# Layer 0's values products in half-block batches, with results held back and value copies moved to ScalarE

## Chip, cores, metric

One core of one Trainium2 chip. The metric is the device time of one launch in microseconds (us), as the median of several runs. Every run in this document is fast, which means that none was over 1.5% above the fastest of the same kernel. Where two kernels are compared by a ratio, it is the mean time of one kernel's fast runs over that of the other's of the same rounds, so it is not quite the ratio of the medians quoted.

## The reference

Two attention layers over eight images of 64 channels and 64 x 64 positions (4,096 positions an image), in fp32.

```python
# layer 0: f and g have 8 channels, h has 64
s = einsum('bci,bcj->bij', f, g);  beta = softmax(s, axis=2)
x = x + einsum('bcj,bij->bci', h, beta)
# layer 1: group norm, then q, k, v of 64 channels
attn = softmax(q @ k.T * 64**-0.5);  x = proj(attn @ v) + x
```

Scores are never stored whole. For each chunk of columns the kernel makes scores, takes their exponentials, multiplies them with the values, keeps the running sum of the exponentials, and divides at the end.

## The kernel before

Each image has four column chunks (`NC`) and sixteen row tiles (`NT`) per chunk in each layer. The order of work is: layer 0 of images 0 and 1 (here "the start"), then layer 1 of image 0, layer 0 of image 2, layer 1 of image 1, and so on. A layer-0 stretch after the start is called a steady phase here; there are six.

PSUM is eight banks of 512 columns. Two of them (0 and 7) take turns as the accumulator of the values products; the other six, and the accumulator's twin while it is free, hold scores. So a layer-0 step works on six or seven score banks:

```python
# one step of layer 0 (cut)
room = list(range(1, 7))
if closed == 0 and taken != BANK:
    room = sorted(room + [free])          # the seventh bank
...
for (k, t, p, h), bank in group:          # TensorE: scores, one bank each
    seq[k][0].scores(banks[:, bank, :], t, p, h, seq[k][1])
...                                       # ScalarE: exponentials, up to four banks each
new += [(k, 2*t + p, e) for ... if h == 1]   # a block: two banks
...
# ended():
for u in due: u[2]()                      # projections, sums, value copies that are due
for r in ready: weigh(*r, now)            # TensorE: values products of the step BEFORE
ready = new
```

A block (`weigh` of layer 0) is two fp32 products of 512 columns into two halves of one bank; each product is two instructions, so a block is four. After every second block, VectorE adds the exponentials to a running sum (`esum`, 2,048 columns, 2.29 us). At a chunk's end come three pieces of work: `sums` (TensorE sums the running sum over partitions, ScalarE copies it, transfers deal it out as `zt`), `reciprocals` (VectorE, then transfers through DRAM to `r`), and `result` (VectorE multiplies by `r`, adds the residual, takes statistics).

Of the kernel before, what the change touches and what calls it, by code (L numbers as in the profile page):

```python
# [19 lines left out]
CW = 512  # L20
# [48 lines left out]
def fast_path(  # L69
# [19 lines left out]
    nc = tc.nc  # L89
    B, C, N = x.shape  # L90
    C8 = WfT.shape[1]
    NH = N // 2
    NC = NH // CW
    NT = NH // P
# [16 lines left out]
    outer = (0, 7)  # L111
    turn = 0
    lent = None

    def pair():
        nonlocal turn
        if lent is not None:
            return pairs[lent]
        turn += 1
        return pairs[turn % 3]  # L120
# [15 lines left out]
    def matmul(*args, **kwargs):  # L136
        in_order(nc.tensor.matmul(*args, **kwargs))  # L137
# [139 lines left out]
    class Attention:  # L277
# [8 lines left out]
        def values(self, src, w, c):  # L286

            ps = pair()
            for t in range(TPC):
                for m in range(2):  # L290
                    for h in range(2):
                        matmul(
                            ps[ts(m, C), h, ts(t, C)], src[ts(h, C), ds(t * P + m * C, C)],
                            w[ts(h, C), :], start=True, stop=True,
                        )
            self.copy_values(  # L296
                self.vt[:, :, ts(c, TPC), :],
                ps[:, :, 0 : TPC * C].rearrange("k p (t c) -> k p t c", c=C),
            )
# [70 lines left out]

    class Layer0(Attention):
        kind = 0
        copy_values = staticmethod(nc.vector.tensor_copy)
        scale = 1.0
        banks = 1

# [62 lines left out]
                ps, self.g[rows, ts(t, P)], self.f[rows, ts(c, CW)], start=True, stop=True  # L439
            )  # L440

        def weigh(self, acc, e, t, p, start, stop):
            for h in range(2):
                matmul(
                    acc[0][ts(h, C), :], self.vt[:, p, t, :], e[:, h, :], start=start, stop=stop
                )

        def total(self, raw, acc):
# [6 lines left out]

    class Layer1(Attention):
        kind = 1
        copy_values = staticmethod(nc.vector.tensor_copy)
        scale = C**-0.5
        banks = 2  # L460

# [93 lines left out]
                        self.parts[ts(h, C), h, ts(c, CW)], start=True, stop=True,  # L555
                    )

        def weigh(self, acc, e, t, p, start, stop):
            for m in range(2):
                for h in range(2):  # L560
                    matmul(
                        acc[m][ts(h, C), :], self.vt[ts(m, C), p, t, :], e[ts(m, C), h, :],
                        start=start, stop=stop,
                    )

        def total(self, raw, acc):
# [19 lines left out]
    seq = [(at, c) for at in order for c in range(NC)]  # L586
# [5 lines left out]
    def at_step(s, work_, takes=PAIR):  # L592
        nonlocal count
        later.append((s, count, work_, takes))
        later.sort(key=lambda u: u[:2])
        count += 1

    def take(s):

        due, taken = [], 0  # L600
        for u in [u for u in later if u[0] <= s]:
            if not (u[3] and taken):
                due.append(u)
                later.remove(u)
                taken = taken or u[3]
        return due, taken
# [9 lines left out]
    for i, at in enumerate(order):  # L616
        if i > 0:

            where = max(k for k in range(i) if order[k].kind == 1 or k == min(i, 2) - 1)
            for s, u, buffer in at.before():  # L620
                at_step(where * NC * NT + s, u, buffer)

    ready = []
    acc = esum = first = None

    def weigh(i, j, e, now):
        nonlocal acc, esum, first
        at, c = seq[i]
        t, p = divmod(j, 2)
        n = f"{at.name}_{c}"  # L630
        if j == 0:
            acc = [banks[:, outer[(c + m) % 2 if at.kind == 0 else m], :] for m in range(at.banks)]
            esum = work.tile([P, 2, 2, CW], F32, tag="esum", name=f"esum_{n}")
        at.weigh(acc, e[:, p], t, p, j == 0, j == 2 * NT - 1)
        if p == 0:
            return
        if t == 0:
            first = e
        else:
            nc.vector.tensor_add(esum, first if t == 1 else esum, e)  # L640
        if t == NT - 1:
            finished(i, now)

    def finished(i, now):

        nonlocal closed
        at, c = seq[i]
        closed = max(closed, 1)
        next_kind = seq[i + 1][0].kind if i + 1 < len(seq) else 1
        works = at.finish(acc, esum, c, i)  # L650
        if len(works) == 1:
            at_step(now, works[0])
            return
        sums, reciprocals, result = works
        delay = 7 if at.kind == 0 else 5
        if at.kind == 1 and c == NC - 2 and i + 2 < len(seq) and seq[i + 2][0].kind == 0:
            delay = NT
        spare = None
        if next_kind == 0:

            spare = outer[c % 2 if at.kind == 0 else 1]
        if at.kind == 1 and c < NC - 1:
            spare = None
        at_step(now + delay, lambda: sums(spare), PAIR if spare is None else BANK)

        layer1 = (i // NC + 1) * NC * NT
        if at.kind == 0 and at.b > 0 and c < NC - 1:
            when = layer1 + 1 + 2 * c
            steps = (when, when + 3)
        else:  # L670

            wait = 4 if next_kind == 0 else 3
            steps = (now + delay + wait, now + delay + 2 * wait)
        at_step(steps[0], reciprocals, 0)
        at_step(steps[1], result, 0)

    closed = 1

    def ended():

        nonlocal ready, closed
        closed = max(closed - 1, 0)
        for u in due:
            u[2]()
            if u[3] == BANK:
                closed = 1
        for r in ready:
            weigh(*r, now)
        ready = new

    i = 0
    while i < len(seq):
        at, c = seq[i]
        if at.kind == 1:
            for j in range(0, 2 * NT, 2):
                now = i * NT + j // 2
                due, taken = take(now)
                t = j // 2
                new = []
                both_ps = [pair(), pair()]  # L700
                for p in range(2):
                    at.scores(both_ps[p], t, p, c)
                e = ppool.tile([P, 2, 2, CW], F32, tag="e", name=f"e_{at.name}_{c}_{t}")
                for p in range(2):
                    nc.scalar.activation(e[:, p], both_ps[p], AF.Exp, scale=at.scale)  # L705
                    new.append((i, j + p, e))
                ended()
            i += 1
            continue

        last = next(k for k in range(i, len(seq) + 1) if k == len(seq) or seq[k][0].kind == 1)
        units = [
            (k, t, p, h)
            for k in range(i, last) for t in range(NT) for p in range(2) for h in range(2)
        ]
        u = 0
        while u < len(units):
            k, t = units[u][:2]
            now = k * NT + t
            due, taken = take(now + 1)  # L720
            if any(j == 0 for _, j, _ in ready):
                closed = max(closed, 1)
            free = outer[1]
            if ready:
                free = outer[(ready[-1][0] + 1) % 2]
                if seq[ready[-1][0]][0].kind == 1:
                    closed = 1
            room = list(range(1, 7))
            if closed == 0 and taken != BANK:
                room = sorted(room + [free])  # L730
            if taken == PAIR:
                lent = 0 if room[-1] == 7 else 2
                room = [r for r in room if r not in (2 * lent + 1, 2 * lent + 2)]
            group = list(zip(units[u : u + len(room)], room))
            u += len(group)
            for (k, t, p, h), bank in group:
                seq[k][0].scores(banks[:, bank, :], t, p, h, seq[k][1])
            new = []
            while group:
                (k, t, p, h), bank = group[0]  # L740
                first_ = 2 * p + h
                n_ = min(4 - first_, len(group))
                at, c = seq[k]
                if first_ == 0:
                    e = ppool.tile([P, 2, 2, CW], F32, tag="e", name=f"e_{at.name}_{c}_{t}")
                nc.scalar.activation(  # L746
                    e.rearrange("k p h n -> k (p h) n")[:, first_ : first_ + n_, :],
                    banks[:, bank : bank + n_, :], AF.Exp, scale=at.scale,
                )
                new += [(k, 2 * t + p, e) for (k, t, p, h), _ in group[:n_] if h == 1]  # L750
                group = group[n_:]
            ended()
            lent = None
        i = last
    now = len(seq) * NT
    for r in ready:
        weigh(*r, now)
# [408 lines left out]
```

## Time and profile before

| | before |
|---|---|
| median of the three runs given with the kernel | 3125.45 us (3122.25 to 3125.78) |
| busy in the trace | TensorE 98%, VectorE 80%, ScalarE 65% |
| from the second layer-0 step to layer 1 of image 0 ("the start") | 326.5 us |
| a steady layer-0 phase, all six | 153.0 us |
| a layer-1 phase, the first six | 229.4 to 229.7 us |
| the rest (layer 1 of images 6 and 7, and the end) | 468.9 us |

The lower four rows are differences between starts of score batches in the trace, each phase cut at the second step of layer 1 and the first of layer 0. TensorE is the engine to follow. Its busy share tells little, because a stalled score batch counts as busy until its last bank is free (0.97 us in place of 0.73 in the timeline that the prediction shows); the lengths of steps tell more.

### The profile page before, as it was taken

Reading aid. Unit: us, or ns where it says so; the run is one execution under the profiler, and the core shown is the slowest. Engines: PE = TensorE matmul, PEld = TensorE weight load, DVE = VectorE, ACT = ScalarE, POOL = GpSimd, SP = SyncE. Lnnn points to the kernel's source line nnn. Section 1 sums busy time; section 2 is a strip of 40 time slices with the busy share of each in tenths; the row PEclk is TensorE's granted clock in tenths of the full one; section 3 lists DMA queues with packets and bytes.
Section 4 is the critical chain, followed back from the end, with each engine's and each line's share of the span. In section 5 each row is a group of like instructions: output and inputs, shape, how many; then the busy total and the mean of one; then the engine's idle time right before and its main releaser. Section 6 shows DMA issues by size and latency. Waiting matters only on the chain.

```text
span 3120.9 us, 58240 instructions
## 1 busy us (share of the span) xinstructions
PE 3070.0 (98%) x25523; PEld 1140.2 (37%) x25523; DVE 2504.3 (80%) x1624; ACT 2042.1 (65%) x1957; POOL 16.5 (1%) x41
## 2 busy tenths in 40 slices
PE   7999999999999999999999999999999999999998
PEld 2332334433344333433334333343333433333433
DVE  6998777798768987689776897769977699776676
ACT  5787655686557865578655785557855588555554
POOL 2000000000000000000000000000000000000000
PEclk9999999999999999999999999999999999999999
DMA  3000010100101001010010100101001000000000
GB/s 84 22 8 18 12 35 18 31 8 8 39 15 32 8 8 39 18 28 8 8 39 18 28 8 8 40 17 32 8 13 40 8 18 8 5 22 15 12 11 12
DMA packets 61814, 63.12 MB, mean 20 GB/s; under 512 B 34944, under 2 KB 35024, under 8 KB 61552
## 3 DMA queue, kind: packets, MB, share of 16 engines
q1 hardware_dynamic: 60432, 59.16, 7.6%
q8 instruction: 202, 3.31, 0.4%
q14 instruction: 60, 0.49, 0.1%
q0 software_dynamic: 800, 0.15, 0.0%
q10 hardware_dynamic: 320, 0.01, 0.0%
HBM read 25.06 MB, written 8.65 MB: 11 GB/s over the span
## 4 chain that ended last, share of the span: by engine, by line
PE 92%; DVE 4%; ACT 2%; issue 1%; DMA 1%; SPq 0%; ACTq 0%; DVEq 0%
PE banks L137 92%; DVE esum_l L640 3%; ACT e_l L746 1%; ACT e_l L705 0%; DMA r_l<-recips 0%; DMA w<-in_WgT_dram 0%; DMA fg_l<-high_l 0%; DVE v_l L296 0%; SPq L334 0%; DVE vt_l L296 0%; DMA zt_l<-zs_l 0%; DVE r_l L359 0%; SPq L431 0%; DMA recips<-stash 0%; DVE high_l L421 0%
## 5 line engine op out<-in xcount | busy, mean ns | idle before, releaser
L640 DVE TENSOR_TENSOR esum_l<-esum_l,e_l 128x2048 f32<-128x2048 f32 x896 | 2051.0, 2289 | 394.1 <-ACT e_l L705 338.4
L705 ACT ACTIVATE e_l<-banks 128x1024 f32<-128x1024 f32 x1024 | 992.9, 1021 | 795.6 <-PE banks L137 763.0
L746 ACT ACTIVATE e_l<-banks 128x2048 f32<-128x2048 f32 (+3 forms) x757 | 954.9, 1325 | 233.2 <-PE banks L137 226.5
L137 PE MATMUL banks<-e_l,v_l 64*64 64x512 f32 (+1 forms) x8704 | 1105.0, 591 | 0.0
L137 PE MATMUL banks<-kq_l 64*64 64x512 f32 (+1 forms) x8448 | 1016.2, 586 | 10.3 <-DVE v_l L296 6.0
L137 PE MATMUL banks<-e_l,vt_l 128*64 128x512 f32 x3584 | 831.6, 601 | 0.7
L137 PEld LDWEIGHTS banks<-e_l,v_l 64*64 64x64 f32 (+1 forms) x8704 | 377.7, 133 | 557.2 <-issue 518.6
L137 PEld LDWEIGHTS banks<-kq_l 64*64 64x64 f32 (+1 forms) x8448 | 367.1, 135 | 576.9 <-issue 522.4
L137 PEld LDWEIGHTS banks<-e_l,vt_l 128*64 128x64 f32 x3584 | 233.0, 136 | 459.0 <-issue 455.3
L137 PE MATMUL banks<-fg_l 32*128 32x512 f32 x1792 | 223.3, 469 | 12.0 <-ACT e_l L746 4.6
L137 PEld LDWEIGHTS banks<-fg_l 32*128 32x128 f32 x1792 | 93.2, 183 | 256.5 <-ACT e_l L746 172.3
L640 DVE TENSOR_TENSOR esum_l<-e_l,e_l 128x2048 f32<-128x2048 f32 x64 | 146.1, 2283 | 22.1 <-ACT e_l L746 12.7
L364 DVE TENSOR_TENSOR raw_l<-raw_l,r_l 128x512 f32<-128x512 f32 x64 | 44.0, 688 | 74.4 <-DMA r_l<-recips 74.4
L137 PE MATMUL banks<-esum_l,ones 128*32 128x512 f32 (+2 forms) x508 | 55.0, 500 | 4.3 <-DVE esum_l L310 2.7
L567 DVE COPY raw_l<-banks 128x512 f32<-128x512 f32 x32 | 22.1, 691 | 33.4 <-PE banks L137 33.4
L345 DVE RECIPROCAL stash<-zt_l 128x8 f32<-128x8 f32 x63 | 12.7, 201 | 40.4 <-DMA zt_l<-zs_l 39.6
L541 ACT ACTIVATE kq_l<-banks,qkb 128x512 f32<-128x512 f32 x64 | 40.6, 696 | 0.0
L310 DVE TENSOR_TENSOR esum_l<-esum_l 128x1024 f32<-128x1024 f32 x32 | 38.9, 1215 | 0.0
L137 PE MATMUL banks<-xn_l,wqk 64*64 64x512 f32 x256 | 33.9, 592 | 0.0
L449 ACT COPY raw_l<-banks 128x512 f32<-128x512 f32 x32 | 19.0, 594 | 19.0 <-PE banks L137 19.0
L329 ACT COPY zs_l<-banks 128x512 f32<-128x512 f32 (+1 forms) x63 | 30.9, 490 | 0.0
L296 DVE COPY v_l<-banks 128x512 f32<-128x512 f32 x36 | 24.7, 686 | 6.6 <-PE banks L137 6.5
(88 smaller groups left out, 387.2 us busy)
## 6 DMA issues: line engine op xcount, KB each, us to landing
r_l<-recips SPq DMA_DIRECT2D x126, 128.0 KB, 2.9
fg_l<-high_l SPq DMA_DIRECT2D x224, 64.0 KB, 2.0
x<-in_x_dram SPq DMA_DIRECT2D x32, 256.0 KB, 4.9
kq_l<-kq_l SPq DMA_DIRECT2D x64, 128.0 KB, 2.3
out_dram<-raw_l SPq DMA_DIRECT2D x64, 128.0 KB, 2.5
kq_l<-high_l SPq DMA_DIRECT2D x32, 64.0 KB, 2.0
zt_l<-zs_l SPq DMA_DIRECT2D x128, 2.0 KB, 1.8
zt_l<-zs_l SPq DMA_DIRECT2D x124, 1.0 KB, 1.7
```

What stands on the lines that cost most here:

```text
L137: in_order(nc.tensor.matmul(*args, **kwargs))
L296: self.copy_values(self.vt[:, :, ts(c, TPC), :], ps[:, :, 0 : TPC * C].rearrange("k p (t c) -> k p t c", c=C),)
L310: nc.vector.tensor_add(esum[:, 0], esum[:, 0], esum[:, 1])
L329: nc.scalar.copy(zs, z[:, 0:width])
L345: nc.vector.reciprocal(rt, zh)
L364: nc.vector.tensor_mul(raw, raw, r)
L449: nc.scalar.copy(raw, acc[0])
L541: nc.scalar.activation(self.parts[:, h, cols], ps[:, h, :], AF.Identity, bias=k1["qkb"][:, h : h + 1],)
L567: nc.vector.tensor_copy(raw, acc[0])
L640: nc.vector.tensor_add(esum, first if t == 1 else esum, e)
L705: nc.scalar.activation(e[:, p], both_ps[p], AF.Exp, scale=at.scale)
L746: nc.scalar.activation(e.rearrange("k p h n -> k (p h) n")[:, first_ : first_ + n_, :], banks[:, bank : bank + n_, :], AF.Exp, scale=at.scale,
```

## The change

The intent: let each layer-0 batch hold exactly as much values work as seven score banks call for (three and a half blocks), stop VectorE from standing in front of TensorE, and hold layer-0 results until layer 1, where VectorE has time. The title's "held" did not exist in effect before: the program asked for it, but the scheduler pulled the ready work forward.

```diff
-            self.copy_values(                      # VectorE
+            copy = nc.vector.tensor_copy if lent is None else nc.scalar.copy
+            copy(                                  # ScalarE inside layer 0
...
+    def due_part(ready):
+        room, now_, left = 7, [], []
+        for k, j, e, cols in ready:
+            size = (cols.stop - cols.start) // (CW // 2)      # half blocks
+            if seq[k][0].kind == 1 or room >= size:
+                now_.append((k, j, e, cols)); room -= size
+            elif room == 1 and 0 < j < 2 * NT - 1:            # split by columns
+                mid = (cols.start + cols.stop) // 2
+                now_.append((k, j, e, slice(cols.start, mid)))
+                left.append((k, j, e, slice(mid, cols.stop)))
+                room = 0
+            else: ...
...
-        if at.kind == 1 and c == NC - 2 and i + 2 < len(seq) and seq[i + 2][0].kind == 0:
-            delay = NT                             # third chunk's sums wait for layer 0
...
+        def behind(work_):
+            def made():
+                with tc.issue_after(added):        # behind the last running-sum add
+                    work_()
+            return made
-        at_step(steps[0], reciprocals, 0)
-        at_step(steps[1], result, 0)
+        at_step(steps[0], behind(reciprocals), 0)
+        at_step(steps[1], behind(result), 0)
...
-        for r in ready:
+        for r in batch:
             weigh(*r, now)
-        ready = new
+        ready = left + new
```

(Shortened, and cut: the column slice passed through `weigh`, and the test that closes the seventh bank, which now looks at the batch.)

More of the change, by code (lines that the diff above doesn't have):

```diff
@@ L372, in fast_path @@
         kind = 0
-        copy_values = staticmethod(nc.vector.tensor_copy)
         scale = 1.0
@@ L440, in scores, with weigh @@
             )
-        def weigh(self, acc, e, t, p, start, stop):
+        def weigh(self, acc, e, t, p, start, stop, cols):
             for h in range(2):
                 matmul(
-                    acc[0][ts(h, C), :], self.vt[:, p, t, :], e[:, h, :], start=start, stop=stop
+                    acc[0][ts(h, C), cols], self.vt[:, p, t, :], e[:, h, cols],
+                    start=start, stop=stop,
                 )
@@ L457, in fast_path @@
         kind = 1
-        copy_values = staticmethod(nc.vector.tensor_copy)
         scale = C**-0.5
@@ L556, in scores, with weigh @@
                     )
-        def weigh(self, acc, e, t, p, start, stop):
+        def weigh(self, acc, e, t, p, start, stop, cols):
             for m in range(2):
@@ L561, in weigh @@
                     matmul(
-                        acc[m][ts(h, C), :], self.vt[ts(m, C), p, t, :], e[ts(m, C), h, :],
-                        start=start, stop=stop,
+                        acc[m][ts(h, C), cols], self.vt[ts(m, C), p, t, :],
+                        e[ts(m, C), h, cols], start=start, stop=stop,
                     )
@@ L624, in fast_path, with weigh @@
     acc = esum = first = None
-    def weigh(i, j, e, now):
-        nonlocal acc, esum, first
+    added = None
+    def due_part(ready):
[3 more added lines that the diff above has]
+            if seq[k][0].kind == 1 or room >= size:
+                now_.append((k, j, e, cols))
+                room -= size
+            elif room == 1 and 0 < j < 2 * NT - 1:
[3 more added lines that the diff above has]
+                room = 0
+            else:
+                left.append((k, j, e, cols))
+                room = 0
+        return now_, left
+    def weigh(i, j, e, cols, now):
+        nonlocal acc, esum, first, added
         at, c = seq[i]
@@ L630, in weigh @@
         n = f"{at.name}_{c}"
-        if j == 0:
+        if j == 0 and cols.start == 0:
             acc = [banks[:, outer[(c + m) % 2 if at.kind == 0 else m], :] for m in range(at.banks)]
             esum = work.tile([P, 2, 2, CW], F32, tag="esum", name=f"esum_{n}")
-        at.weigh(acc, e[:, p], t, p, j == 0, j == 2 * NT - 1)
-        if p == 0:
+        at.weigh(acc, e[:, p], t, p, j == 0, j == 2 * NT - 1, cols)
+        if p == 0 or cols.stop < CW:
             return
@@ L639, in weigh @@
         else:
-            nc.vector.tensor_add(esum, first if t == 1 else esum, e)
+            added = nc.vector.tensor_add(esum, first if t == 1 else esum, e).ins
         if t == NT - 1:
@@ L697, in fast_path @@
                 due, taken = take(now)
+                batch, left = ready, []
                 t = j // 2
@@ L705, in fast_path @@
                     nc.scalar.activation(e[:, p], both_ps[p], AF.Exp, scale=at.scale)
-                    new.append((i, j + p, e))
+                    new.append((i, j + p, e, slice(0, CW)))
                 ended()
@@ L720, in fast_path @@
             due, taken = take(now + 1)
-            if any(j == 0 for _, j, _ in ready):
-                closed = max(closed, 1)
+            batch, left = due_part(ready)
             free = outer[1]
-            if ready:
-                free = outer[(ready[-1][0] + 1) % 2]
-                if seq[ready[-1][0]][0].kind == 1:
-                    closed = 1
+            if batch:
+                free = outer[(batch[-1][0] + 1) % 2]
+                if seq[batch[-1][0]][0].kind == 1 or any(b[1] == 0 for b in batch):
+                    closed = max(closed, 1)
             room = list(range(1, 7))
@@ L749, in fast_path @@
                 )
-                new += [(k, 2 * t + p, e) for (k, t, p, h), _ in group[:n_] if h == 1]
+                new += [
+                    (k, 2 * t + p, e, slice(0, CW)) for (k, t, p, h), _ in group[:n_] if h == 1
+                ]
                 group = group[n_:]
```

## The prediction

> **What bounds the kernel now.** I read the page first: busy shares, then the chain that ended last.
>
> ```profile
> PE 3070.0 (98%) x25523; PEld 1140.2 (37%) x25523; DVE 2504.3 (80%) x1624; ACT 2042.1 (65%) x1957; POOL 16.5 (1%) x41
> ...
> PE 92%; DVE 4%; ACT 2%; issue 1%; DMA 1%; SPq 0%; ACTq 0%; DVEq 0%
> ```
>
> TensorE carries 92% of the chain, and the other 8% (some 250 us) is partly start, end and semaphore hops. So the question is only how much TensorE waiting the change can remove. The change touches layer 0, so I next read the timeline of a steady layer-0 stretch, by engine (start, length, group).
>
> ```profile
> 614.49 0.98 PE L137 MATMUL banks<-fg_l 32*128 32x512 f32 x7
> 615.40 3.65 PE L137 MATMUL banks<-e_l,vt_l 128*64 128x512 f32 x16
> ...
> 618.98 0.73 PE L137 MATMUL banks<-fg_l 32*128 32x512 f32 x7
> 619.56 3.23 ACT L746 ACTIVATE e_l<-banks 128x1536 f32<-128x1536 f32 x2 [1.22 <-PE banks L137]
> 619.65 2.80 PE L137 MATMUL banks<-e_l,vt_l 128*64 128x512 f32 x12
> 622.37 0.97 PE L137 MATMUL banks<-fg_l 32*128 32x512 f32 x7
> 623.28 3.65 PE L137 MATMUL banks<-e_l,vt_l 128*64 128x512 f32 x16
> 623.37 3.22 ACT L746 ACTIVATE e_l<-banks 128x2048 f32<-128x2048 f32 x2 [0.58 <-PE banks L137]
> ```
>
> A step is a batch of seven score products, then a batch of values products from the step before. Seven banks are three and a half blocks, so whole blocks alternate 3 (12 instructions) and 4 (16). Score start to score start gives 3.39 us (618.98 to 622.37) and 4.49 us (to 626.86). A block is four instructions, two at a time side by side; 3.65 - 2.80 = 0.85 us, from finer readings 0.857. A step of 3 is then 0.82 + 3 x 0.857 = 3.39 us, where 0.82 is the scores and both changes of tile shape. A step of 4 should be 0.82 + 4 x 0.857 = 4.25 us, but takes 4.49: 0.24 us too much. It sits in its score batch, 0.97 instead of 0.73: ScalarE ends the seven exponentials at 619.56 + 3.23 = 622.79, 0.42 us after the scores began, and the last scores wait for those banks. So there is one stall of 0.24 us wherever a full score batch follows a full score batch with a short values batch.
>
> The busy times by stretch show how close VectorE is, in two pieces of the start and in one steady phase (start and end, length, then busy time of each engine).
>
> ```profile
> core 0: us, PE busy (x) PEld busy (x) DVE busy (x) ACT busy (x) POOL busy (x), PEclk, DMA share, GB/s
> ...
> 137.00:235.00 98.00, 97.71 (x555) 31.96 (x553) 93.78 (x54) 80.88 (x66) 0.00 (x0) 1.00 0.02 7
> 235.00:352.40 117.40, 110.47 (x698) 35.16 (x694) 104.59 (x83) 86.59 (x77) 0.00 (x0) 0.97 0.07 17
> ...
> 592.00:739.40 147.40, 146.82 (x800) 46.47 (x798) 142.15 (x81) 120.33 (x102) 0.00 (x0) 1.00 0.08 21
> ```
>
> VectorE is busy 96%, 89% (the piece with the stalls) and 96% of them, so it runs late, and anything queued on it in layer 0 comes late. The value copies are such a thing. The timeline of the worst one:
>
> ```profile
> 259.97 9.46 DVE L640 TENSOR_TENSOR esum_l<-esum_l,e_l 128x2048 f32<-128x2048 f32 x4
> ...
> 262.26 0.69 PE L137 MATMUL banks<-wvp,xn_l 64*64 64x64 f32 x32
> ...
> 269.35 0.68 DVE L296 COPY v_l<-banks 128x512 f32<-128x512 f32 x1
> 270.09 0.79 PE L137 MATMUL banks<-kq_l 32*128 32x512 f32 x2 [3.97 <-DVE v_l L296]
> 270.81 3.68 PE L137 MATMUL banks<-e_l,v_l 128*64 128x512 f32 x8
> ```
>
> The products are ready at 262.95, but four adds stand before their copy; TensorE sits 3.97 us for the bank. Then eight values products take 3.68 us, where two blocks take 1.94 elsewhere.
>
> **What the Trainium skill says.** "TensorEngine Tiling (Array Packing)", Key Properties: changing the tiling mode drains TensorE. The trace agrees: a layer-0 step pays 0.82 us beside its values products, while a layer-1 step, all in one shape (64 rows by 64 columns), takes 3.43 us for 32 instructions, just 8 slots of 0.43. Halving a block adds no change of shape. "TensorE: Matmul & The Clock Gate", part 1: an idle window of about 3.4 us can drop the clock to half. The trace agrees: after the 3.97 us wait the same work took nearly double, and that stretch alone shows a clock of 0.97. The same page, "Engine queue depths": ScalarE and VectorE are strict first-in first-out. It agrees with the copy that waited behind four adds.
>
> **The change, part by part**, with the built order of instructions of both kernels. There are two layer-0 images at the start, then six phases of one layer-0 image, each followed by layer 1. Steps and score counts are the same in both builds.
>
> (1) Batches of 3.5. The changed order has 85 halved blocks. A step of 3.5 should take 0.82 + 3.5 x 0.857 = 3.82 us; ScalarE is done 0.57 + 3.22 = 3.79 us after the scores began, so the next scores' second half, starting at 4.06, waits for nothing. Total TensorE work is the same; only stalls go. Not all of them: a first or last block is never halved, and at chunk seams 3-block batches stay. In a steady phase, full-after-full with a short batch occurs 11 times before and 6 times after: 5 x 0.24 = 1.2 us saved. At the phase's two ends, I step through by the same figures: the first four steps take 13.48 us now and, with 0.857 us of values moved there from the end, 14.34; about 13.95 by the new order. The last three save 0.46 (the 0.46 us wait for ScalarE before layer 1 falls away, as the last score batch is five). So 1.2 + 0.4 + 0.45 = 2.05 us a phase. The halves cost more instructions: 32 values-projection matmuls of 64 columns take 0.62 us, 78 ns a slot, 25 ns more than streaming alone (0.428 / 8 = 53 ns). Two more slots a halving: 85 x 2 x 0.025 = 4 us at worst; I take 2, since weight loads (0.14 us a pair) fit inside a slot of 0.21.
>
> (2) The sums of a layer-1 third chunk move from the first layer-0 step into layer 1. Such sums cost 0.73 us in layer 1 when the partial sums are ready (810.64 to 814.80, 4.16 against 3.43), and 1.15 where VectorE has just had a copy, a normalisation and the totals (869.89, 4.58). The third chunk has that heavier set: +1.15 us a phase; what it frees is in the 0.4 above. Net of (1) and (2): -0.9 us, times six: -5.4 us.
>
> (3) Results of three chunks held. Now the scheduler pulls them forward into layer 0. In the new order they stand behind adds of the next layer 1. A set costs 0.36 + 0.69 + 0.75 + 0.69 = 2.5 us of VectorE, so 7.5 us a phase leaves a VectorE with some 5 us idle in 147. In steady phases TensorE is not seen waiting for VectorE, so it saves nothing directly. In layer 1, VectorE has 1.14 us free a step (3.43 - 2.29), some 13.7 us in twelve steps against 10 us of held work: it fits.
>
> (4) Value copies by ScalarE, eight of them, all in the start. I compared every start step with 0.82 + 0.857 a block + 1.0 for sums or a projection + 0.62 for a values projection. The sum from 30.48 to 352.39 us is 321.9 us against 298.7, so 23 us are stalls. Those on copies: 1.9 (113.05), 1.5 (129.23), 0.4 (138.13), 6.3 (265.62, with its slow clock) and 1.1 (311.13), about 11 us. The rest: 1.4 for a transfer at 37.5, about 4.3 after 2-block steps (ScalarE not done), and short-batch stalls. After: 15 short-batch stalls x 0.24 = 3.6; after 2-block and 2.5-block steps 3 x 1.1 + 2 x 0.65 = 4.6; the transfer 1.4 and the first projection 0.7; I allow 2 for VectorE lateness that shows elsewhere. That is 12.3 in place of 23: -11 us. The copy costs ScalarE about 0.6 us (its raw copy: 594 ns), in steps where it has five banks (2.37 us) instead of seven.
>
> Sum: -11 - 5.4 + 2 = -14.4 us; 3125.45 - 14.4 = **3111 us**, 0.5% faster.
>
> **Rivals.** *VectorE was the hidden bound of layer 0*, at 96%: then moving 7.5 us a phase saves up to 6 x 5 = 30 us more, 3080. For it: adds run back to back. Against: steady steps fit TensorE's own sum, the only excess being the 0.24 from ScalarE. *A half costs as much as a whole*: four half slots a halving, each 0.214 us too long, 85 x 4 x 0.214 = +73 us, about 3184. Against: 64-column slots take 78 ns, so slots do scale with columns. *The held results clog VectorE in layer 1*: a result waits there for its broadcast (reciprocal and product stand only two adds apart, about 6.9 us, with 2.9 us for the landing), adds fall behind, exponentials wait for buffers. At 2 us a phase: +12 us, about 3123. For it: idle before the product on that transfer is 74.4 us over the run. *The stall only moves*: without the copy wait, the late adds at 235 to 270 us hold the exponentials' buffers and half of the 11 us stays: 3116.
>
> **Range and chances.** A steady phase (586.40 to 739.43) takes 153.0 us against 148.8 by the same sum, so all stalls I can find are about 23 + 6 x 4.2 = 48 us, 1.5%, so over 2% faster is nearly shut out. Slower by 2% needs the second rival. Range 3097 to 3121 us: the low end is the start freed entirely and the halves free, plus some of the first rival; the high end has the third and fourth together. Chances: faster 0.02, within 2% 0.97, slower 0.01.
>
> **What would show it.** Right: steady steps of 3.82 us with a 0.73 us score batch after them; six 0.24 us stalls a phase; no wait for the values copies between 100 and 340 us; the clock at 1.00 throughout the start; VectorE busy about 139 us of a layer-0 phase; the layer-1 phase about 1.1 us longer. Wrong: steps of 3.5 clearly over 3.82 (halves cost), TensorE or ScalarE waiting on the running-sum adds in layer 1, or a gain in steady phases above 3 us each (VectorE mattered).

## The result

The changed kernel takes 3106.16 us (median of 4 runs, 3105.62 to 3106.77) against 3124.52 us (4 runs). The ratio is 0.9942, interval 0.9925 to 0.9959: 0.6% faster, within the predicted range, 5 us below the predicted time. The page's busy shares and chain:

```profile
PE 3063.5 (99%) x25863; PEld 1122.5 (36%) x25863; DVE 2506.6 (81%) x1616; ACT 2045.5 (66%) x1976; POOL 16.7 (1%) x41
...
PE 96%; DVE 1%; ACT 1%; issue 1%; SPq 0%; DMA 0%; ACTq 0%; DVEq 0%
```

TensorE's share of the chain went from 92% to 96%, and VectorE's from 4% to 1%. TensorE has 340 more instructions and is busy 6.5 us less, which is waiting that used to be counted as busy. The timeline of a steady phase (start, length, engine, group):

```profile
600.91 0.73 PE L137 MATMUL banks<-fg_l 32*128 32x512 f32 x7
601.48 3.22 ACT L776 ACTIVATE e_l<-banks 128x1536 f32<-128x1536 f32 x2 [0.79 <-PE banks L137]
601.57 3.23 PE L137 MATMUL banks<-e_l,vt_l 128*64 128x256 f32 x16
604.73 0.74 PE L137 MATMUL banks<-fg_l 32*128 32x512 f32 x7
...
605.40 3.23 PE L137 MATMUL banks<-e_l,vt_l 128*64 128x512 f32 x16
...
608.56 0.73 PE L137 MATMUL banks<-fg_l 32*128 32x512 f32 x7
```

Both steps take 3.82 us (600.91 to 604.73, 604.73 to 608.56: 3.83), and both later score batches take 0.73 to 0.74 us. The sixteen instructions of a values batch are now twelve of full width and four of half width (the view prints one shape for a mixed group), and take 3.23 us, between the 2.80 and 3.65 of before. ScalarE is done at 604.70, just before the next scores begin. The copy that had cost TensorE 3.97 us, in the timeline of the same place:

```profile
259.50 0.69 PE L137 MATMUL banks<-wvp,xn_l 64*64 64x64 f32 x32
260.13 2.37 PE L137 MATMUL banks<-e_l,v_l 128*64 128x256 f32 x12
261.63 0.59 ACT L298 COPY v_l<-banks 128x512 f32<-128x512 f32 x1
262.43 0.73 PE L137 MATMUL banks<-kq_l 32*128 32x512 f32 x6
```

ScalarE copies at 261.63, 1.4 us after the products end, while TensorE is at its values batch; the next scores wait for nothing. The busy times by stretch (columns as in the prediction's view). The first two are the prediction's stretches, the second cut where layer 1 now begins; the third is the same phase, from its first layer-0 step to its first layer-1 step:

```profile
137.00:235.00 98.00, 97.80 (x576) 33.79 (x570) 94.15 (x55) 80.67 (x71) 0.00 (x0) 1.00 0.03 7
235.00:341.60 106.60, 105.46 (x711) 35.53 (x707) 95.27 (x62) 86.09 (x77) 0.00 (x0) 1.00 0.05 11
575.90:722.90 147.00, 146.57 (x852) 49.65 (x848) 139.82 (x66) 122.40 (x103) 0.00 (x0) 1.00 0.05 12
```

The clock of the second stretch is 1.00 where it was 0.97. VectorE in the steady phase is busy 139.82 of 147.00 us. The prediction's 142.15 of 147.40 is not of the same cut: that stretch begins 5.6 us after the phase's first step and ends inside layer 1. Cut alike (586.40 to 733.97), the kernel before had 141.08 of 147.57, so the fall is only 1.3 us. Results left the phase, but VectorE runs behind and filled most of the time with running-sum adds: 59 begin in the phase, 57 before. Where the 16.8 us of the two profiled spans went (3120.9 to 3104.1), by phase:

| phase | before | after | difference in all |
|---|---|---|---|
| the start | 326.5 | 315.3 | -11.3 |
| steady layer-0 phases, six | 153.03 | 151.62 | -8.4 |
| layer-1 phases, first six | 229.40 to 229.68 | 230.14 | +4.0 |
| the rest | 468.9 | 467.8 | -1.1 |

### The profile page after: what moved, and what is told of

Its sections match the earlier page's. It is cut to its first block, busy times and chain, and to the rows that moved or that the text cites. A ratio compares the mean times of both kernels' runs of the same rounds, so it can differ in the third digit from the quotient of the medians.

```text
span 3104.1 us, 58905 instructions
## 1 busy us (share of the span) xinstructions
PE 3063.5 (99%) x25863; PEld 1122.5 (36%) x25863; DVE 2506.6 (81%) x1616; ACT 2045.5 (66%) x1976; POOL 16.7 (1%) x41
## 4 chain that ended last, share of the span: by engine, by line
PE 96%; DVE 1%; ACT 1%; issue 1%; SPq 0%; DMA 0%; ACTq 0%; DVEq 0%
PE banks L137 96%; DVE esum_l L662 1%; ACT e_l L776 1%; SPq L432 0%; ACT e_l L736 0%; DMA w<-in_WgT_dram 0%; DMA x<-in_x_dram 0%; DVE vt_l L298 0%; DVE r_l L361 0%; DVE high_l L422 0%; DMA fg_l<-high_l 0%; ACTq L169 0%; DVE raw_l L366 0%; DVE esum_l L312 0%; ACT full_l L417 0%
## 5 line engine op out<-in xcount | busy, mean ns | idle before, releaser
L137 PE MATMUL banks<-e_l,vt_l 128*64 128x512 f32 (+1 forms) x3884 | 831.5, 567 | 0.0
L137 PEld LDWEIGHTS banks<-e_l,v_l 64*64 64x64 f32 (+1 forms) x8744 | 360.0, 133 | 576.0 <-issue 534.0
L137 PEld LDWEIGHTS banks<-kq_l 64*64 64x64 f32 (+1 forms) x8448 | 348.7, 134 | 579.3 <-issue 544.6
L137 PEld LDWEIGHTS banks<-e_l,vt_l 128*64 128x64 f32 x3884 | 254.3, 136 | 470.4 <-issue 457.0
L137 PE MATMUL banks<-x,wfg 64*64 64x512 f32 x128 | 19.0, 640 | 9.7 <-DVE low L179 9.3
L137 PEld LDWEIGHTS banks<-wh,x 64*64 64x64 f32 x1024 | 22.0, 135 | 15.7 <-issue 13.3
L137 PEld LDWEIGHTS banks<-wvp,xn_l 64*64 64x64 f32 x1024 | 20.6, 134 | 16.8 <-issue 16.8
```

Of the source, the lines that this page charges most:

```text
L137: in_order(nc.tensor.matmul(*args, **kwargs))
```

## The experiments

All of them gave correct results. "Before" is 3123.6 us in the runs of the first eight experiments (e1 to e6, h1 and h2) and 3124.3 us in those of the last three (e7 to e9), which ran on another chip: compare those with the others by their phases. The phases of their traces:

| run | median us | ratio to before | start | layer 1, first six | steady layer 0 | rest |
|---|---|---|---|---|---|---|
| changed kernel | 3106.16 | 0.9942 | 315.3 | 230.14 | 151.62 | 467.8 |
| e1_whole_blocks | 3113.58 | 0.9967 | 316.4 | 230.1 to 230.5 | 152.53 | 468.6 |
| e2_copies_vector | 3114.00 | 0.9967 | 320.8 | 230.1 to 230.5 | 151.62 | 468.7 |
| e3_not_held | 3115.24 | 0.9973 | 314.9 | 230.3 to 232.9 | 151.61 | 470.3 |
| e4_delay_back | 3104.40 | 0.9938 | 314.9 | 229.40 | 151.98 | 467.8 |
| e5_all_halved | 3108.18 | 0.9949 | 315.1 | 230.13 | 152.04 | 468.6 |
| e6_copies_alone | 3113.02 | 0.9966 | 316.4 | 229.4 to 229.6 | 153.01 | 469.0 |
| e7_held_alone | 3121.63 | 0.9988 | 326.5 | 229.40 | 153.01 | 468.3 |
| e8_not_held_delay_back | 3109.81 | 0.9953 | 314.3 | 229.4 to 231.4 | 151.97 | 470.1 |
| e9_halves_alone | 3115.10 | 0.9969 | 322.1 | 229.4 to 231.4 | 151.97 | 469.1 |
| h1_matched | 3093.76 | 0.9903 | 311.0 | 230.13 | 150.20 | 468.1 |
| h2_matched_delay | 3090.59 | 0.9893 | 310.9 | 229.40 | 150.51 | 469.1 |

The first layer-0 step ends (the second begins) between 30.1 and 31.7 us in all of them; a difference of less than about 1.5 us between two spans may be that alone. The half intervals of the ratios are about 0.0015, some 4.5 us, so small differences are read from the phases.

### e1_whole_blocks: no halves

```diff
-            batch, left = due_part(ready)
+            batch, left = ready, []
```

> The changed kernel with whole blocks in every batch; all else as changed. Theory (ScalarE's seven exponentials outlast a 3-block batch, 0.24 us a time): about 10 such stalls a steady layer-0 phase in place of 6, so a steady phase 1.0 us longer, the start some 2 us longer: +8 us on 3106, about 3114; steps of 3.39 and 4.49 us come back. Rival (the gain comes from VectorE being relieved, halving is worth nothing): 3106, steady phase unchanged at 151.6 us.

Measured 3113.58 us, a steady phase of 152.53 us (+0.91), the start 1.2 us longer. The stalls are back, seen in TensorE's timeline:

```profile
602.53 0.73 PE L137 MATMUL banks<-fg_l 32*128 32x512 f32 x7
603.19 2.80 PE L137 MATMUL banks<-e_l,vt_l 128*64 128x512 f32 x12
605.92 0.96 PE L137 MATMUL banks<-fg_l 32*128 32x512 f32 x7
```

The score batch behind a 3-block batch takes 0.96 us again, and the built order has ten such places a phase against six. The trace of the first steady phase shows 12 score batches over 0.85 us against 8 in the changed kernel, the stretched second step left out; some of these have six banks, which the count of the built order leaves out. The difference is four either way: 4 x 0.24 = 0.96, and 0.91 was measured. The theory holds, and the rival (halving is worth nothing) falls.

### e2_copies_vector: copies back on VectorE

```diff
-            copy = nc.vector.tensor_copy if lent is None else nc.scalar.copy
+            copy = nc.vector.tensor_copy
```

> The changed kernel with the eight value copies of the start back on VectorE. Theory (TensorE waits for a bank whose copy stands behind adds): only the start grows; 6 to 11 us longer between its first step (30.5 us) and the first layer-1 step (341.6 us), waits for a copy of v_l visible again; 3112 to 3117. Rival (the copies only showed VectorE's lateness, which the held results have cured): start within 2 us, 3106 to 3108.

Measured 3114.00 us; the start is 5.6 us longer and no steady phase moves (another 1.2 us lie before the start, 0.35 in one layer-1 phase and 0.9 in the rest, none touched by the edit). TensorE's waits for a copy of `v_l` are back in the start, 5.1 us in all (8.5 before, none in the changed kernel). So the copies' part is real, but with the other parts in place it is 5.6 us, just under the 6 to 11 us expected.

### e3_not_held: the scheduler may pull results forward again

```diff
-        at_step(steps[0], behind(reciprocals), 0)
-        at_step(steps[1], behind(result), 0)
+        at_step(steps[0], reciprocals, 0)
+        at_step(steps[1], result, 0)
```

> The changed kernel without the rule that puts reciprocals and results behind the last add: the scheduler pulls them into layer 0 again. Theory (TensorE does not wait for VectorE in steady layer 0): steady phase within 0.3 us of 151.6, VectorE in it about 7 us busier; start longer by 0 to 3 us; 3106 to 3109. Rival (VectorE at 96% was the hidden bound): steady phase at least 1 us longer each, start 5 us longer, 3116 or more.

Measured 3115.24 us, just under the rival's 3116, but not where the rival put it. The steady phases are 151.61 us, equal to the changed kernel's, although VectorE has results in them again: the theory's own sentence holds, and the results in layer 0 cost TensorE nothing. (VectorE is busy 141.52 of 147.04 us, only 1.7 more than in the changed kernel and not the 7 expected, as it does one add fewer.) The start is not longer either. The 9 us are in layer 1: its six phases take 0.1 to 2.8 us more each (7.0 together), and the rest 2.5. The total falls outside what the theory expected; holding does matter, for a reason neither theory had. VectorE's waits for transfers, one line of each kernel's list (waiter, what it waited for: us in all, times, longest), first of the kernel before, then of this run:

```profile
DVE raw_l L364 <- DMA r_l<-recips: 74.4, 28, 4.4
```

```profile
DVE raw_l L366 <- DMA r_l<-recips: 95.4, 32, 4.3
```

The changed kernel has no such line. VectorE takes its work in order (the prediction cites the page that says so), so while the product waits for `r`, everything behind it waits, and in layer 1 a value copy that TensorE needs can be behind it. The held rule puts the reciprocal and the product behind adds that are later in the program, by which time the transfers have landed. The chain of waits of this run runs through `zt`, `recips` and `r` in each of the phases that grew by over half a microsecond. The transfer that is late differs: `zt` at 481.31 (3.43 us, 1.7 is the median), `recips` at 1631.51 (2.82 us, mostly 1.39), `r` at 2459.65 (3.97 us, 2.9 is the median).

### e4_delay_back: the third chunk's sums back in layer 0

```diff
         delay = 7 if at.kind == 0 else 5
+        if at.kind == 1 and c == NC - 2 and i + 2 < len(seq) and seq[i + 2][0].kind == 0:
+            delay = NT
```

> The changed kernel with the sums of layer 1's third chunk back in the first layer-0 step. Theory: the layer-1 phase loses the 0.74 us that the change added, the layer-0 phase gains about as much at its first steps: -0.5 to +0.5 us a pair, 3103 to 3109. Rival (moving the sums freed the layer-0 start, most of the steady gain of 1.4 us a phase): +1.4 us less 0.7 a pair, about 3111.

Measured 3104.40 us. Layer-1 phases are 229.40 us again (-0.74) and steady layer-0 phases 151.98 (+0.36), the same in each of the six. So this part of the change costs 0.38 us a phase, 2.3 us in all; the theory holds. The medians differ by 1.8 us and their ratios' intervals overlap; the phases carry the verdict.

### e5_all_halved: what a half costs

```diff
-        for r in batch:
-            weigh(*r, now)
+        for k, j, e, cols in batch:
+            if seq[k][0].kind == 0 and 0 < j < 2 * NT - 1 and cols == slice(0, CW):
+                weigh(k, j, e, slice(0, CW // 2), now)
+                weigh(k, j, e, slice(CW // 2, CW), now)
+            else:
+                weigh(k, j, e, cols, now)
```

> The changed kernel with every layer-0 values block that is neither first nor last of its chunk halved by columns (the two halves right after each other), some 850 more halvings, about 1,700 more slots of half width. Theory (a slot costs in proportion to its columns, weight loads fit beside it): 3106, plus at most 4 us. Rival (a fixed 25 ns a slot, as 64-column products would suggest): +43 us, 3149. Rival (a half costs a whole): over 3700 us.

The built order has 960 halved blocks in place of 85. Measured 3108.18 us; a steady phase is 0.42 us longer with 109 more halvings, so a halving costs about 4 ns. Both rivals fall. The weight loads double too, and stay beside the products.

### e6_copies_alone: the kernel before with ScalarE copies only

```diff
-            self.copy_values(
+            copy = nc.vector.tensor_copy if lent is None else nc.scalar.copy
+            copy(
```

> The kernel before with only the eight value copies of the start moved to ScalarE. Theory: nothing changes after the start (steady phases 153.03 us, layer-1 phases 229.4); the start, 326.5 us from its second step to layer 1, shrinks by 8 to 11 us, so 3113 to 3116. Rival (the lateness of VectorE shows at once in other waits): the start shrinks by 5 us or less, 3119 or more.

Measured 3113.02 us; the start shrinks from 326.5 to 316.4 us, and nothing else moves by more than 0.2 us a phase. The theory holds: -10.2 us from this part alone.

### e7_held_alone: the kernel before with the held rule only

```diff
-            nc.vector.tensor_add(esum, first if t == 1 else esum, e)
+            added = nc.vector.tensor_add(esum, first if t == 1 else esum, e).ins
...
-        at_step(steps[0], reciprocals, 0)
-        at_step(steps[1], result, 0)
+        at_step(steps[0], behind(reciprocals), 0)
+        at_step(steps[1], behind(result), 0)
```

> The kernel before with only the rule that puts reciprocals and results behind the last add. Theory (VectorE's waits for landings go, from 74 us for r_l to near 0, but in the kernel before TensorE hardly stood for them): steady phases 153.0 us, layer-1 phases 229.4, start 0 to 3 us shorter: 3120 to 3124. Rival (its 9 us of the run without it are its own worth): 3115 or less.

Measured 3121.63 us, ratio 0.9988 (interval 0.9975 to 1.0002). All layer-1 phases are 229.40 us (in the kernel before, two had 0.1 and 0.3 more), the start and the steady phases are as before, and the rest is 0.6 us shorter. Its worth alone is about 1 us in the traces; the theory holds.

### e8_not_held_delay_back: neither held nor early sums

```diff
+        if at.kind == 1 and c == NC - 2 and i + 2 < len(seq) and seq[i + 2][0].kind == 0:
+            delay = NT
...
-        at_step(steps[0], behind(reciprocals), 0)
-        at_step(steps[1], behind(result), 0)
+        at_step(steps[0], reciprocals, 0)
+        at_step(steps[1], result, 0)
```

> The changed kernel without the rule and with the sums of layer 1's third chunk back in layer 0. Theory (not holding costs only together with the early sums, which put one more wait for two landings into layer 1, in front of a value copy): layer-1 phases 229.4 to 229.7, total 3104 to 3107. Rival (holding is worth its 9 us in any order): 3112 or more.

Measured 3109.81 us, between the two expectations: a miss for both. Against e4_delay_back, which differs by the held rule alone, it is 5.4 us slower: two of six layer-1 phases have 2.0 and 1.9 us more, and the rest 2.3. So without the early sums the loss is less common, but not gone. One of the two phases, in the timeline:

```profile
485.59 0.20 DVE L347 RECIPROCAL stash<-zt_l 128x8 f32<-128x8 f32 x1 [3.83 <-DMA zt_l<-zs_l]
...
491.08 0.69 DVE L366 TENSOR_TENSOR raw_l<-raw_l,r_l 128x512 f32<-128x512 f32 x1 [3.11 <-DMA r_l<-recips]
...
492.48 4.68 DVE L662 TENSOR_TENSOR esum_l<-esum_l,e_l 128x2048 f32<-128x2048 f32 x2
...
497.07 0.68 DVE L298 COPY v_l<-banks 128x512 f32<-128x512 f32 x1
...
497.81 1.52 PE L137 MATMUL banks<-kq_l 64*64 64x512 f32 x12 [1.74 <-DVE v_l L298]
```

VectorE idles 3.83 us for `zt` and 3.11 us for `r`; two adds and then the value copy come behind; TensorE stands 1.74 us for the copy. In the kernel before, the same two waits took 1.68 and 2.40 us, and TensorE did not stand. Why was `zt` late? The transfers of this kernel in the window 481.5 to 485.5 us (queue and kind: packets, MB, share; then the issues with their median time to landing):

```profile
q8 instruction: 1, 0.02, 1.4%
...
zt_l<-zs_l SPq DMA_DIRECT2D x2, 1.0 KB, 2.8
```

The last of the four `zt` transfers, issued at 481.58, landed at 485.46, 3.9 us later, where 1.7 is the median. An instruction packet of 16 KB (0.93 us long) ran at 483.45, between issue and landing. I counted this over five traces (before, changed, e3, e8, e9), for the 1,119 `zt` transfers of 1,260 whose landing the traces tell: of 47 that took over 2.6 us, 43 had such a packet between issue and landing; of the 1,072 others, 17. The changed kernel has one at nearly the same place (`zt` issued at 481.54, landed at 484.80), and VectorE's timeline there shows what the held rule does with it:

```profile
483.93 2.29 DVE L662 TENSOR_TENSOR esum_l<-esum_l,e_l 128x2048 f32<-128x2048 f32 x1 [2.22 <-ACT e_l L736]
486.14 0.20 DVE L347 RECIPROCAL stash<-zt_l 128x8 f32<-128x8 f32 x1
```

The reciprocal stands behind an add and waits for nothing. By the same count the changed kernel has the most late `zt` transfers of the five (15; 9 in e3_not_held, 10 in e8_not_held_delay_back), and all six of its layer-1 phases are 230.14 us.

### e9_halves_alone: the kernel before with halves only

The function `due_part`, the column slices and the closing test as in the change's diff, and nothing else:

```diff
+            batch, left = due_part(ready)
...
-        for r in ready:
+        for r in batch:
             weigh(*r, now)
-        ready = new
+        ready = left + new
```

> The kernel before with only the halved blocks. Theory: steady phases shorter by about 5 x 0.24 = 1.2 us, the start by 1 to 5 us, layer-1 phases unchanged: 3111 to 3116. Rival (VectorE, 96% busy without the other parts, holds TensorE back and eats the gain): steady phases within 0.4 us of 153.0.

Measured 3115.10 us; the steady phases are 151.97 us (-1.06), the start 4.5 us shorter. The theory holds there, with VectorE still carrying the results; "layer-1 phases unchanged" missed: two have 1.6 and 2.0 us more, of the kind seen in e8_not_held_delay_back.

### h1_matched: a better fit of batches

The six remaining stalls a phase come from steps with six banks, which the change lets eat seven half blocks if there are as many, so that a later full step has only three blocks. This version takes as many half blocks as the step has banks:

```diff
-    def due_part(ready):
-        room, now_, left = 7, [], []
+    def due_part(ready, room=7):
+        now_, left = [], []
...
+            if len(room) < 7:
+                batch, left = due_part(ready, len(room))
             group = list(zip(units[u : u + len(room)], room))
```

> The changed kernel, but a step with fewer than seven score banks also takes only as many half blocks of values as it has banks, so a full score batch always has 3.5 blocks beside it. The built order has one full-after-full with a short batch a steady phase in place of six, two in the start in place of fifteen. Theory (0.24 us each): steady phases 151.6 - 1.2 = 150.4 us, the start 3 to 5 us shorter: 3093 to 3096. Rival (the stalls move to other steps because ScalarE is the bound over a longer stretch): 3102 or more.

Measured 3093.76 us (ratio 0.9903); steady phases 150.20 us (-1.42) and the start 4.2 us shorter. The theory holds.

### h2_matched_delay: both

```diff
+            if len(room) < 7:
+                batch, left = due_part(ready, len(room))
...
+        if at.kind == 1 and c == NC - 2 and i + 2 < len(seq) and seq[i + 2][0].kind == 0:
+            delay = NT
```

> The same, and the sums of layer 1's third chunk back in the first layer-0 step, which alone was worth some 2 us on the changed kernel. Theory: both add up, layer-1 phases 229.4 us, 3091 to 3095. Rival: the matched batches lose at the first layer-0 steps what the layer-1 phase saves, 3094 to 3097, no better than without.

Measured 3090.59 us (3090.20 to 3091.28) against 3093.76 (3093.51 to 3093.98) of h1_matched: both add up. TensorE's timeline:

```profile
613.12 0.73 PE L137 MATMUL banks<-fg_l 32*128 32x512 f32 x6
613.78 2.80 PE L137 MATMUL banks<-e_l,vt_l 128*64 128x512 f32 x12
616.51 0.74 PE L137 MATMUL banks<-fg_l 32*128 32x512 f32 x7
```

A six-bank step takes three blocks (3.39 us), and the full one behind it does not stall. At 0.9893 of before (interval 0.9878 to 0.9908), this version beats both kernels: 1.1% and, by medians, 0.5%.

## Why the prediction was right

The time fell inside the range, and the sum of -14.4 us stands against -16.8 us between the profiled spans (-18.4 between the medians). That it came so near is partly luck: the gain in the steady phases was put 3.9 us too high (12.3 for 8.4), and the charges for the moved sums and the halves 2.9 and 1.7 us too high, which about cancels; 1.1 us of gain in the rest was not forecast.

- **Step lengths and the stall of 0.24 us: right.** 3.82 us was forecast for a 3.5-block step and 3.82 measured; e1_whole_blocks brought the stalls back in number and size.
- **Steady phases: the mechanism right, the size off.** Predicted -2.05 us a phase; measured -1.41. The order's six stalls became eight: a six-bank batch behind a full step with three blocks can stall as well (0.93 us at 585.91 and 1.02 at 688.04 in place of 0.73), and my count took full batches only. These two make some 0.5 of the 0.64 us that are missing. The first of them lies in the first four steps, which took 14.18 us and not 13.95; the last three saved 0.45 us, as said.
- **The moved sums: right in kind.** +1.15 us predicted for a layer-1 phase, +0.74 measured (4.24 us for such a step against 3.43, with the partial sums ready sooner than at the second chunk). Net of the two terms I said -5.4 us and got -4.4 (-8.4 + 4.0). e4_delay_back shows that this part alone is a loss of 2.3 us, which I had folded into a net and not named.
- **The start: right in total, its split not.** -11 us predicted, -11.3 measured, all put on the copies. Alone the copies give -10.2 (e6_copies_alone) and the halves -4.5 (e9_halves_alone); together with the rest -11.3. The two overlap: with all else changed, taking the copies back costs only 5.6 us. The clock recovered to 1.00 as said. That VectorE's lateness "shows elsewhere" by 2 us is neither shown nor excluded.
- **Cost of halves: too high.** I took 2 us for 85; e5_all_halved puts a halving at about 4 ns, so 0.3 us.
- **VectorE's relief: read from two cuts.** "VectorE busy about 139 us" came (139.82), but from 141.08 on the same cut: taking the results out of layer 0 left VectorE nearly as busy as before, since it runs behind and its adds fill the time.
- **"So it saves nothing directly" (the held results): the step that failed in part.** For layer 0 it was right: 151.62 us with the rule and 151.61 without. But the changed kernel needs the rule: without it, 9 us of the gain go in layer 1 and at the end (e3_not_held), through in-order waits for late landings in the places that I looked at. In the kernel before the same waits were there (74.4 us for `r` alone), and cost TensorE little, which is why the rule alone is worth about 1 us (e7_held_alone). I had read the 74.4 us as an argument for the rival that held results would clog layer 1; they were an argument for holding.
- **The rivals.** VectorE as the hidden bound of layer 0 falls (e3_not_held, and e9_halves_alone with its load in place). A half at the cost of a whole falls. Clogging in layer 1 falls: 230.14 us in every phase is the moved sums. A stall that only moves falls: copies alone took 10.2 us off the start.

What stays open: why the late landings fall on such different places from kernel to kernel. The link with instruction packets is a count over traces, and of `zt` alone, not an experiment; no run changed where those packets fall.

## What to carry to other kernels

When two engines alternate over a shared buffer, look at each step's own length against the other engine's, and not at averages: uneven batches pay the slower side in one step and the faster side's idle time is not given back. Cut the work finer than the buffer's unit if the finer cut is free (measure it by cutting everything), and match each batch to the step it runs beside. An in-order engine that only "waits for a transfer" while off the critical path carries a risk for anything critical that is queued behind it; ordering the wait behind other work removed it here and cost nothing (e7_held_alone, which has the rule alone, is no slower than the kernel before).

## What the Trainium skill lacked or had wrong

- "TensorEngine Tiling (Array Packing)", Instruction Overhead, gives each matmul about 60 cycles of overhead. Read as a cost added to every matmul, that doesn't hold here: cutting 512-column products into 256-column ones added about 4 ns a block (four more instructions, two side by side), 0.42 us for 109 halvings.
- The same page, Key Properties, says that a mode switch drains TensorE, but gives no size. Here a layer-0 step pays 0.82 us beside its values products; with two score slots of about 0.23 us (0.73 against 0.50 us for seven and four banks), some 0.36 us are left for both switches and whatever else is paid once a batch (an estimate from these durations).
- "Runtime: NRT & Kernel Launch", Instruction fetch mechanics, says that instructions are fetched in 16 KiB blocks while the program runs, and calls the cost mostly hidden. What it lacks is that small transfers of the kernel can land late beside such a fetch. The traces show about 200 packets of 16 KB a run (202 before, 204 after), some 1 us long (0.97 and 1.10 us, medians), and 43 of 47 late landings of `zt` (over 2.6 us against a median of 1.7) with one between issue and landing.
- "TensorE: Matmul & The Clock Gate", part 1, on the clock halving after an idle window, agreed: a wait of 3.97 us, then 3.68 us for work of 1.94, and a clock of 0.97 in that stretch; 1.00 once the wait was gone.
